# Graph attention with a residual norm on one core: the output bias of the last two tiles added by VectorE, the last tile's power by itself

## The chip, the cores and the metric

The kernel runs on one core of one Trainium2 chip. The metric is the device time of one execution in microseconds (us); the time before is the median of five runs.

## The reference

There are 16 graphs of 1024 nodes with 512 features, one adjacency matrix for all of them, and 8 heads of 64. Cut to what matters:

```python
q = (x @ Wq + bq).reshape(b, n, H, HD)        # k and v likewise
scores = jnp.einsum('bqhd,bkhd->bhqk', q, k) / jnp.sqrt(jnp.float32(HD))
scores = scores + (1.0 - adj)[None, None, :, :] * -1000000000.0
attn = jax.nn.softmax(scores, axis=-1)
out = jnp.einsum('bhqk,bkhd->bqhd', attn, v).reshape(b, n, d)
y = x + out @ Wo + bo
result = (y - mean(y)) / sqrt(var(y) + 1e-5)  # over the 512 features
```

## The kernel before

Nodes are sorted by degree and cut into 8 tiles of 128 queries, for each of 16 graphs: 128 tiles in all. Keys and values are gathered only where the adjacency has an edge, in 560 blocks of 128 rows (35 for each graph). The instructions are issued in an order that the program writes out itself: a loop over steps n (L1097 to L1175), in which each block takes its turn, and in which functions are set down for a later step (`later` puts them in `plan`, `later_last` in `rest`). `total` is the number of blocks, 560, so steps with n of 560 or more lie behind the last block. `fronts` is the list of the projections (q, k, v) still to be done; it runs empty some steps ahead of the last graph. An engine works through its own list in that order, and nothing overtakes.

What this text follows is the end of a tile:

- `normalise` (L977) divides the weighted sum by the denominator; TensorE transposes it (`poT`, L1002), and ScalarE copies it to `oT` (L1006). Ten tiles of two earlier graphs are put off to the end: their `oT` lies in HBM (`spill`) and comes back by `reload` (L773) as `oTs`, for the time when no projections are left.
- `load_y` (L762) brings the residual rows into `Y`, for the late tiles by a DMA on SyncE's queue (L769).
- `finish` (L779) makes the output product `po`: four units, each one matmul of 128x512 in float32 (`product`, L578 to L589). The profile shows each such matmul as two passes, so a tile's product is 8 passes on line L584. When no projections are left (`biased`), a fifth unit goes in after the second: a matmul of a column of ones with the bias `bo_bc` (L868 to L873), 2 passes more on line L869.
- `out` (L784) adds product and residual on VectorE and sums the row in the same instruction (L799); while there are projections an own instruction (L798) adds the product, and L799 the bias. Then, each at its step: `centre` (VectorE, L804), `spread` (ScalarE, squares, L808), `variance` (VectorE, L811), the power to -0.5 (GpSimd), `shift` (VectorE, L817), `norm_out` (ScalarE, L820) and `store` (GpSimd, an indirect DMA to the sorted places, L824).
- The power of a tile is an instruction of its own while there are projections (`power`, L814, 128x1). After that two tiles share one of 128x2 (`powers`, L841): the second of a pair calls it, and both shifts follow it. A first tile that gets no mate is finished by `alone` (L857), which is set down for 6 steps after its `out`.

The last two tiles to be finished are tile 7 of graph 13 (a put-off one, with `oTs`) and then tile 7 of graph 15. Between them, VectorE and TensorE work off the guard's last part (L1056 to L1070: two reductions over `ends`, three small instructions, a transpose `pgt` on TensorE at L1065, and three more that write `flag`). Every engine loads `flag` at the end (L1177) and branches past the general version, which does not run here.

In the last stretch VectorE's list reads: `ends` (L1018, twice), the two shifts of the pair before (L817), L799 of tile 13/7, the guard's instructions, L804 and L811 of tile 13/7, L799 of tile 15/7 and its L804, L811 and the two L817.

Of the kernel before, what the change touches and what calls it, by code (L numbers as in the profile page):

```python
# [14 lines left out]
OP = mybir.AluOpType  # L15
# [145 lines left out]
def kernel(  # L161
# [36 lines left out]
    nc = tc.nc  # L198
# [21 lines left out]
    bo_bc = const.tile([P, D], F32, name="bo_bc")  # L220
# [8 lines left out]
    with ExitStack() as main:  # L229
# [120 lines left out]
        now, plan, rest, urgent = [0], {}, {}, []  # L350

        def later(k, fn):
            plan.setdefault(now[0] + k, []).append(fn)

        def later_last(k, fn):
            rest.setdefault(now[0] + k, []).append(fn)
# [185 lines left out]
        X, XT, SX, KV, VSUM, NRM, Y, OT, PS = {}, {}, {}, {}, {}, {}, {}, {}, {}  # L542
# [35 lines left out]
        def product(name, lhs, w, out):  # L578

            def unit(c):  # L580
                if c == 0:
                    PS[name] = fill_psum(name)
                p = PS[name]
                nc.tensor.matmul(p, lhs()[:, ts(c, P)], w[:, c, :], start=(c == 0), stop=(c == NPAIR - 1))  # L584
                if c == NPAIR - 1:
                    del PS[name]
                    later(1, lambda: out(p))

            return [(PRODUCT, lambda c=c: unit(c), None) for c in range(NPAIR)]  # L589
# [189 lines left out]
        def finish(b, t):  # L779


            biased = not fronts

            def out(p):  # L784
                OT.pop((b, t))
                y = Y[b, t]

                if fronts:
                    st = small.tile([P, 5], F32, name="stats", bufs=6)
                else:  # L790

                    second = bool(half)
                    if not second:
                        half.append([small.tile([P, 2, 5], F32, name="stats_2", bufs=3)])
                    st2 = half[0][0]
                    st = st2[:, int(second), :]
                if not biased:
                    nc.vector.tensor_tensor(y, p, y, op=OP.add)  # L798
                nc.vector.scalar_tensor_tensor(  # L799
                    y, p if biased else bo_bc, 1.0, y, op0=OP.mult, op1=OP.add, accum_out=st[:, 0:1]  # L800
                )

                def centre():
                    nc.vector.tensor_scalar(st[:, 1:2], st[:, 0:1], -1.0 / D, None, op0=OP.mult)  # L804

                def spread():
                    sq = work.tile([P, D], F32, tag="ysq", name=f"ysq_{b}_{t}", bufs=1)
                    nc.scalar.activation(sq, y, AF.Square, bias=st[:, 1:2], accum_out=st[:, 2:3])  # L808

                def variance():  # L810
                    nc.vector.tensor_scalar(st[:, 2:3], st[:, 2:3], 1.0 / D, EPS, op0=OP.mult, op1=OP.add)  # L811

                def power():
                    nc.gpsimd.tensor_tensor(st[:, 3:4], st[:, 2:3], neg_half, op=OP.pow)  # L814

                def shift():
                    nc.vector.tensor_tensor(st[:, 4:5], st[:, 3:4], st[:, 1:2], op=OP.mult)  # L817

                def norm_out():
                    nc.scalar.activation(y, y, AF.Identity, bias=st[:, 4:5], scale=st[:, 3:4])  # L820
                    later(2, store)

                def store():
                    nc.gpsimd.indirect_dma_start(  # L824
                        out=out_rows[b, t], out_offset=bass.IndirectOffsetOnAxis(ap=asked_row[:, t:t + 1], axis=0),
                        in_=y, in_offset=None, element_offset=b * N * D,
                    )
                    del Y[b, t]

                later(1, centre)  # L830
                later_last(2, spread)
                later(3, variance)
                if fronts:
                    later(4, power)
                    later(5, shift)
                    later_last(6, norm_out)
                elif second:
                    mate_shift, mate_norm_out = half.pop()[1]

                    def powers():  # L840
                        nc.gpsimd.tensor_tensor(  # L841
                            st2[:, :, 3:4], st2[:, :, 2:3], neg_half[:, :, None].to_broadcast([P, 2, 1]), op=OP.pow
                        )

                    def shifts():
                        mate_shift()
                        shift()

                    later(4, powers)
                    later(6, shifts)  # L850
                    later_last(6, mate_norm_out)
                    later_last(7, norm_out)
                else:
                    mine = half[0]
                    mine.append((shift, norm_out))

                    def alone():  # L857
                        if half and half[0] is mine:
                            half.pop()
                            power()  # L860
                            later(2, shift)
                            later_last(3, norm_out)

                    later(6, alone)

            units = product(f"po_{b}_{t}", lambda: OT[b, t], W["o"], out)
            if biased:
                def bias():  # L868
                    nc.tensor.matmul(  # L869
                        PS[f"po_{b}_{t}"], ident[:, 0:1].to_broadcast([P, P]), bo_bc, start=False, stop=False  # L870
                    )

                units.insert(2, (PRODUCT, bias, None))  # L873
            return units
# [198 lines left out]
        done, coming, spilled, gathered, fronts, guarded = [], [], [], [0], [], []  # L1073

        total = len(blocks)
# [7 lines left out]
        with tc.manual_schedule():  # L1083
# [13 lines left out]
            while n < total or plan or rest or urgent or done or finishing or spilled or not guarded:  # L1097
# [45 lines left out]
                while credit > 0 or urgent:  # L1143
                    if urgent and not (first_unit and fronts):
                        urgent.pop(0)()
                        continue
                    if (
                        not finishing and len(done) > (LAZY if fronts else 0) and n > loaded.get(done[0], n) + 1
                        and n > last_finish + 1 and not total - 2 <= n < total
                    ):  # L1150
                        finishing = finish(*done.pop(0))
                        last_finish = n
                    units = finishing or fronts
                    if not units:
                        if urgent:
                            urgent.pop(0)()
                            continue
                        break
                    cost, fn, ready = units[0]
                    if ready and not ready():  # L1160
                        if urgent:
                            urgent.pop(0)()
                            continue
                        break
                    del units[0]
                    fn()
                    credit -= cost
                    first_unit = False
# [41 lines left out]
```

## Time and profile before

| what | value |
|---|---|
| median of five runs | 1997.37 us (1994.44 to 1999.51) |
| the profiled execution's own time | 2002.05 us |
| its span, first to last instruction | 2000.2 us |
| mean granted TensorE clock | 0.989 |
| TensorE busy | 1919.3 us, 96% of the span |
| VectorE busy | 1783.9 us, 89% |
| ScalarE busy | 1555.2 us, 78% |
| GpSimd busy | 1296.9 us, 65% |

In the profile PE is TensorE's matmuls, PEld its weight loads, DVE is VectorE, ACT is ScalarE, POOL is GpSimd and SP is SyncE; a "q" behind the name is the engine's sequencer. Times are us from the start of the span unless ns is written. In the list of instructions in order of time, a row gives the start, the time from the first start to the last end, the engine, the line, the operation and its tiles, how many were merged ("x4"), and in brackets the idle time ahead of it and what ended that. In the chain of waits, which is followed back from the last instruction, a row gives the start, the length of that piece of the chain, and whose it is.

### The profile page before, as it was taken

To read this page: it belongs to the slowest core of one execution; us is meant where nothing else is said; L and a number is where in the kernel's file an instruction comes from. 1 tells how busy PE (TensorE), PEld (TensorE's weight loads), DVE (VectorE), ACT (ScalarE), POOL (GpSimd) and SP (SyncE) were. 2 spreads that over 40 slices of the span, in tenths; PEclk is the share of its full clock that TensorE was granted. 3 is DMA by queue.
4 is the path that set the end of the run, shared out by engine and by line. 5 is a ranking of instruction groups with operands and counts; after the bars stand their busy time and mean duration, and the time that the engine had idled before them with its cause. 6 is when DMAs were issued, how large, how long until landed. Compare 5 with 4: busy or idle time off the path is not lost.

```text
span 2000.2 us, 25754 instructions
## 1 busy us (share of the span) xinstructions
PE 1919.3 (96%) x5379; PEld 924.2 (46%) x5379; DVE 1783.9 (89%) x3754; ACT 1555.2 (78%) x6096; POOL 1296.9 (65%) x1205
## 2 busy tenths in 40 slices
PE   8987999999999999999999999999999999889895
PEld 4433454444545454454545445454444545444442
DVE  3788989989899989999998999999799999999895
ACT  3525878878797888879887887979788788878794
POOL 1662565856767686767767686767657675556784
PEclk9999999999999999999999999999999999999998
DMA  6796887888879788888878788888878888988984
GB/s 247 220 340 230 264 304 241 301 270 274 320 260 325 246 295 289 300 290 277 304 260 312 267 304 278 291 302 266 285 257 283 294 303 312 322 280 263 334 308 142
DMA packets 191140, 563.10 MB, mean 282 GB/s; under 512 B 31711, under 2 KB 31739, under 8 KB 190974
## 3 DMA queue, kind: packets, MB, share of 16 engines
q0 software_dynamic: 121632, 403.22, 60.9%
q1 hardware_dynamic: 66736, 153.16, 20.7%
q10 hardware_dynamic: 2606, 4.99, 0.7%
q14 instruction: 122, 1.00, 0.2%
q8 instruction: 44, 0.72, 0.1%
HBM read 442.25 MB, written 143.71 MB: 293 GB/s over the span
## 4 chain that ended last, share of the span: by engine, by line
PE 79%; DVE 10%; issue 4%; DMA 3%; ACT 2%; POOL 1%; POOLq 0%; SPq 0%; DVEq 0%; ACTq 0%
PE po L584 19%; PE pq L584 18%; PE pp L698 13%; PE x L698 9%; PE z L698 9%; PE pxT L555 2%; PE poT L1002 2%; DVE qk L925 2%; PE sum L975 2%; PE sum L974 2%; DVE s L929 2%; DMA kvg<-kv_rows,key_row 1%; ACT pv L949 1%; DVE pv L965 1%; PE pm L646 1%
## 5 line engine op out<-in xcount | busy, mean ns | idle before, releaser
L904 POOL DMA_INDIRECT kvg<-kv_rows,key_row x560 | 636.2, 1136 | 445.6 <-ACT pv L949 116.1
L949 ACT ACTIVATE pv<-kvg,pv 128x64 f32<-128x64 f32 x3552 | 894.7, 339 | 0.5 <-issue 0.4
L584 PE MATMUL pq<-wq,xT 128*128 128x512 f32 x1024 | 480.5, 599 | 3.9 <-issue 1.7
L584 PE MATMUL po<-wo,oT 128*128 128x512 f32 x944 | 438.6, 597 | 4.2 <-DVE y L798 1.9
L929 DVE TENSOR_REDUCE s<-qk 128x8 f32<-128x512 f32 x560 | 380.3, 679 | 6.0
L925 DVE TENSOR_TENSOR qk<-qt,kvg 128x512 f32<-128x512 f32 x464 | 316.9, 683 | 8.3 <-DMA kvg<-kv_rows,key_row 5.0
L584 PEld LDWEIGHTS pq<-wq,xT 128*128 128x128 f32 x1024 | 191.5, 191 | 223.1 <-issue 207.2
L584 PEld LDWEIGHTS po<-wo,oT 128*128 128x128 f32 x944 | 176.2, 191 | 207.3 <-issue 193.2
L698 PE MATMUL pp<-t,s 128*128 128x512 f32 x504 | 237.3, 593 | 8.0 <-DVE s L570 7.0
L698 PE MATMUL x<-b,xT 128*128 128x512 f32 x504 | 237.6, 594 | 0.0
L965 DVE TENSOR_TENSOR pv<-pv,pv 128x520 f32<-128x520 f32 x336 | 232.5, 692 | 0.0
L939 ACT ACTIVATE pv<-s,absent 128x8 f32<-128x8 f32 x464 | 135.6, 293 | 111.0 <-DVE s L929 66.0
L824 POOL DMA_INDIRECT out_dram<-y,asked_row x128 | 149.9, 1171 | 38.8 <-issue 27.3
L888 POOL DMA_INDIRECT qt<-q_rows,asked_row x128 | 142.6, 1114 | 36.7 <-issue 34.8
L594 ACT ACTIVATE sq_k<-kv 128x128 f32<-128x128 f32 x512 | 150.7, 299 | 10.2 <-DVE kv L721 9.0
L698 PEld LDWEIGHTS pp<-t,s 128*128 128x128 f32 x504 | 94.7, 190 | 117.4 <-issue 106.6
L698 PEld LDWEIGHTS x<-b,xT 128*128 128x128 f32 x504 | 95.2, 191 | 113.6 <-issue 109.9
L752 POOL DMA_INDIRECT y<-in_x_dram,asked_row x102 | 115.2, 1129 | 30.6 <-issue 30.0
L698 PE MATMUL z<-b,s 128*128 128x512 f32 x252 | 120.4, 601 | 5.9 <-DVE kv L726 5.9
L898 POOL DMA_INDIRECT qg<-q_rows,query_row x96 | 106.9, 1113 | 27.2 <-issue 24.9
L698 PE MATMUL z<-t,s 128*128 128x512 f32 x252 | 118.7, 593 | 0.1
L698 PE MATMUL pp<-t,xT 128*128 128x512 f32 x252 | 118.4, 592 | 0.0
(194 smaller groups left out, 2613.7 us busy)
## 6 DMA issues: line engine op xcount, KB each, us to landing
kv_rows<-kv SPq DMA_DIRECT2D x128, 512.0 KB
x<-in_x_dram SPq DMA_DIRECT2D x128, 256.0 KB
q_rows<-q SPq DMA_DIRECT2D x128, 256.0 KB
kvg<-kv_rows,key_row POOLq DMA_INDIRECT x560
residual<-y_sorted SPq DMA_DIRECT2D x26, 256.0 KB
y<-residual SPq DMA_DIRECT2D x26, 256.0 KB
adj<-in_adj_dram POOLq DMA_DIRECT2D x8, 512.0 KB
spill<-oT SPq DMA_DIRECT2D x10, 256.0 KB
```

The lines of the kernel that those rows point to most:

```text
L584: nc.tensor.matmul(p, lhs()[:, ts(c, P)], w[:, c, :], start=(c == 0), stop=(c == NPAIR - 1))
L594: nc.scalar.activation(sq, s[:, ts(h, P)], AF.Square, scale=scale, accum_out=sums[:, h:h + 1])
L698: nc.tensor.matmul(R[bank], l[:, ts(c, P)], right[:, c, :], start=(first and c == 0), stop=(c == 1), skip_group_check=True,)
L752: nc.gpsimd.indirect_dma_start(out=y, out_offset=None, in_=x_rows, in_offset=bass.IndirectOffsetOnAxis(ap=asked_row[:, t:t + 1], axis=0), ...
L824: nc.gpsimd.indirect_dma_start(out=out_rows[b, t], out_offset=bass.IndirectOffsetOnAxis(ap=asked_row[:, t:t + 1], axis=0), in_=y, in_offse ...
L888: nc.gpsimd.indirect_dma_start(out=QT[b, t], out_offset=None, in_=q_rows[b % ROWS], in_offset=bass.IndirectOffsetOnAxis(ap=asked_row[:, t: ...
L904: nc.gpsimd.indirect_dma_start(out=KG[n], out_offset=None, in_=kv_rows[b % ROWS], in_offset=bass.IndirectOffsetOnAxis(ap=key_row[:, g:g + ...
L925: nc.vector.tensor_tensor(QK[n], q, KG[n][:, 0:D], op=OP.mult)
L929: nc.vector.tensor_reduce(S[n], QK.pop(n).rearrange("p (h d) -> p h d", d=HD), axis=AX.X, op=OP.add)
L939: nc.scalar.activation(PV[n][:, D:], S.pop(n), AF.Exp, bias=bias)
L949: nc.scalar.activation(pv[:, ts(h, HD)], v[:, ds(D + h * HD, HD)], AF.Copy, scale=pv[:, D + h:D + h + 1])
L965: nc.vector.tensor_tensor(PV[b, t], PV[b, t], pv, op=OP.add)
```

## The change

Behind the last block (step n at or past `total` when `finish` is called) the bias matmul is left out, and VectorE adds `bo_bc` to the residual in `Y` at that moment, which is ahead of the product in the order of the program. L799 then adds the product, as before. A tile whose `out` comes later than step `total + 3` gets its own statistics tile, its own power (L814) and the steps of a single tile.

```diff
         def finish(b, t):
-            biased = not fronts
+            biased = not fronts and now[0] < total
+
+            if now[0] >= total:
+                nc.vector.tensor_tensor(Y[b, t], Y[b, t], bo_bc, op=OP.add)
+
+            fronts_then = bool(fronts)
 
             def out(p):
                 OT.pop((b, t))
                 y = Y[b, t]
 
-                if fronts:
+                single = fronts or now[0] > total + 3
+                if single:
                     st = small.tile([P, 5], F32, name="stats", bufs=6)
                 else:
...
-                if not biased:
+                if fronts_then:
                     nc.vector.tensor_tensor(y, p, y, op=OP.add)
                 nc.vector.scalar_tensor_tensor(
-                    y, p if biased else bo_bc, 1.0, y, op0=OP.mult, op1=OP.add, accum_out=st[:, 0:1]
+                    y, bo_bc if fronts_then else p, 1.0, y, op0=OP.mult, op1=OP.add, accum_out=st[:, 0:1]
                 )
...
-                if fronts:
+                if single:
                     later(4, power)
                     later(5, shift)
                     later_last(6, norm_out)
```

In the lists of instructions that the two programs give their engines, this is all that differs, and it touches the last two tiles alone. TensorE loses the bias matmul of tile 13/7 and that of tile 15/7. VectorE gains an add for each (L785 of the changed kernel): that of 13/7 between L1018 and the two L817 of the pair before, that of 15/7 between the instruction that writes `flag` and L811 of tile 13/7. GpSimd has two powers of 128x1, first that of 13/7 and then that of 15/7, in place of one of 128x2, and both still stand ahead of the last two stores. Tile 15/7 is now normalised (L820) and stored ahead of 13/7; before, 13/7 came first. The lists of ScalarE and SyncE hold the same instructions. The finished tile 13/7 is the first of a pair without a mate, and `alone` finishes it.

## The prediction

> **What bounds the kernel now.** I read the list of instructions that the change moves first, since everything up to about 1973 us is the same program on every engine: only what lies behind that can be won or lost. Then I read, of the profile before, the chain of waits over the last 40 us, the instructions in order of time, the rows of the instructions that come and go, the DMA view around the residual's loads, and last the table of stretches for the granted clock.
>
> The chain of waits tells which engine the end hangs on:
>
> ```profile
> 1973.30 1.72 PE po L584 x4
> 1975.02 0.86 PE po L869 x2
> 1975.88 1.73 PE po L584 x4
> ...
> 1977.63 0.70 DVE y L799 x2
> ...
> 1979.13 0.25 PE pgt L1065
> 1979.38 1.72 PE po L584 x4
> 1981.10 0.86 PE po L869 x2
> 1981.96 1.73 PE po L584 x4
> ...
> 1983.71 0.71 DVE y L799 x2
> ...
> 1985.84 0.72 POOL stats L841
> ```
>
> Three things are to be seen. Both output products are on the chain whole, the bias passes among them. Between them the chain goes over VectorE (L799 of tile 13/7, then the guard's five small instructions) and the guard's transpose on TensorE, so the second product starts when the guard lets it, and that starts from the first product's end. Behind the second product comes a thread with one instruction at a time, in which the power on GpSimd has its whole length.
>
> VectorE's own instructions in order of time, over the same stretch:
>
> ```profile
> 1974.85 0.34 DVE L1018 TENSOR_REDUCE ends<-rden 128x1 f32<-128x64 f32 x2
> ...
> 1977.63 0.69 DVE L799 SCALAR_TENSOR_TENSOR y<-po,y 128x512 f32<-128x512 f32 x1 [2.30 <-PE po L584]
> ...
> 1983.71 0.69 DVE L799 SCALAR_TENSOR_TENSOR y<-po,y 128x512 f32<-128x512 f32 x1 [3.46 <-PE po L584]
> ```
>
> Ahead of each L799 VectorE sat idle, 2.30 and 3.46 us, and the product ended the wait. That is the room for the two adds.
>
> **The bias passes.** Each tile loses two passes, on the chain 0.86 us (the weight loads behind these passes start 0.43 us apart too, so this is not only a modelled end). The first product is the last to arrive at L799, so L799 of 13/7 starts at 1977.63 - 0.86 = 1976.77. The guard's chain follows it unchanged, and the guard's transpose ends at 1979.38 - 0.86 = 1978.52. The second product also needs the copy `oT` (L1006): TensorE's transpose `poT` starts at 1977.43 - 0.86 = 1976.57, takes 0.60, and ScalarE's copy at 0.59 ends about 1977.8, still 0.7 us ahead of the guard. So the second product runs from 1978.52 and takes 3.45 in place of 4.31: it ends at 1981.97, before at 1983.69. **Sum of both: 1.72 us**, all on the chain.
>
> **The first add.** The trace has no add of residual and bias, so its price is bounded by the adds of two 128x512 operands in SBUF that it does have: L994 takes 0.691 at the least, 0.692 in the median, 0.764 at most. I take 0.69. It starts behind L1018 at about 1975.1 and ends at 1975.8. Queued behind it are the two L817 (0.22), then L799: VectorE is free at 1976.0, 0.75 us ahead of the product at 1976.77. The L817 release ScalarE's L820 of tile 15/6 (0.81), which moves from 1975.29 to about 1976.0 and ends at 1976.85; the `oT` copy stands behind it and can't start before 1977.2 anyway. So the add costs nothing on the chain; without this cover it would cost at most its own 0.69 to 0.76, and it can't gain, since nothing it replaces was on VectorE.
>
> The add also brings a wait forward: the residual is wanted at 1975.1, where L799 wanted it at 1977.63. SyncE issued the last two residual loads between 1964.96 and 1965.76, and the DMA view shows traffic of SyncE's queue kind only until about 1969; between 1969.5 and 1975 there is none. So the rows lay there 6 us early, and the wait is nought.
>
> **The second add** stands between the write of `flag` and L811 of 13/7, at about 1979.2 to 1979.9. Behind it wait L811 of 13/7 (which releases the first of the two powers, 4 us before the second needs GpSimd) and L799 of 15/7 at 1981.99. Hidden by the product, with 1.9 us to spare; uncovered it would cost 0.7.
>
> **The power.** Two rows price it:
>
> ```profile
> L814 POOL TENSOR_TENSOR stats<-stats,neg_half x106: 556/587/2062, 224.5 to 1858.6; 128x1 f32<-128x1 f32 x106
> ```
>
> ```profile
> L841 POOL TENSOR_TENSOR stats<-stats,neg_half x11: 717/910/1250, 1882.3 to 1985.8; 128x2 f32<-128x2 f32 x11
> ```
>
> (ns, least, median, most.) Both grow when VectorE is busy beside them; behind the second product it is idle, and there the pair took the least, 0.72. The single one should take its least as well: 0.56. The power of 13/7 goes ahead, at about 1980, where GpSimd is idle. So 0.72 - 0.56 = **0.16 us** less on the chain; from both sides, 0.16 gained and, with the median 0.587 or a stretch such as 0.87 (the last L814 of the run), 0.13 gained to 0.15 lost. I take 0.16, from the row that is as quiet as the tail.
>
> The order of the last two tiles after it (15/7 first) is symmetric: the same shifts, the same two L820, the same two stores in one queue, one step apart as before. Nothing for it. The stretch of 10 us from the last store's issue (1990.20) to the end of the span holds its landing and the program's end and stays.
>
> **Sum.** 1.72 + 0.16 = 1.88 us. Of the profiled execution: 2002.05 - 1.88 = 2000.2, its span 1998.3. That execution lies 4.7 us above the median of the runs; since the tail has no part that differs between executions that I can see, I take the same 1.88 from the median: **1995.5 us**, 0.09% less. The runs differ by 5 us among themselves, and a difference under 0.2% (4 us) can hardly be told from no change: that is the bound for the chances below.
>
> **A rule against the change.** While L994 ran (1974.24 to 1974.93, two operands in SBUF) a store's issue was on GpSimd from 1973.94 to 1974.97; L994 took 0.69 as everywhere. The Trainium skill, SBUF — State Buffer, in "Who interferes with whom", says that a VectorE instruction with two SBUF inputs contends with a GpSimd instruction that reads SBUF, and the later one is blocked whole. By the rule the first add, if it came second to a store's issue, would wait for its end (1976.25); by the row it would not wait. By the rule the sum would be 1.88 - 0.4 = 1.5 us.
>
> **The rivals.**
>
> First, the add is not hidden: it starts only when GpSimd's store issue (1975.28 to 1976.25) is through. It ends at 1976.95, the L817 at 1977.15, and L799 starts 0.4 us after the product. The guard and the second product move with it: 1.88 - 0.4 = 1.5, **1995.9 us**. For it speaks that L841 took up to 1.25 with VectorE busy, so the two do disturb each other; against it that the L994 beside an issue kept its 0.69.
>
> Second, the change doesn't do on the second product what it says: the time won ahead of it is lost waiting for ScalarE's copy, because the add delays L817, so L820, so the copy. Then only one product's 0.86 and the power's 0.16 remain: 1.0 us, **1996.4 us**. It needs the copy to end at 1979.38 in place of 1977.8, 1.6 us late, and L820's delay is 0.7, of which 0.35 is idle time of ScalarE anyway. Little speaks for it.
>
> Third, slower: the clock. The change takes work from TensorE ahead of a gap (1.1 us for the guard). The table of stretches, cut into windows of 3.41 us, the step in which the granted clock changes here (columns: window, its length, busy time and count of PE, PEld, DVE, ACT, POOL, granted clock, DMA share, GB/s):
>
> ```profile
> 1887.04:1890.45 3.41, 0.58 (x3) 0.16 (x1) 3.38 (x9) 0.46 (x3) 3.03 (x3) 1.00 0.96 329
> 1890.45:1893.86 3.41, 1.53 (x6) 1.03 (x7) 3.34 (x16) 2.08 (x10) 2.49 (x4) 0.50 0.90 347
> ...
> 1975.79:1979.20 3.41, 2.33 (x10) 1.09 (x9) 1.39 (x8) 1.45 (x3) 1.43 (x2) 1.00 0.52 199
> ```
>
> A window with 0.58 us of matmuls was followed by one at half clock; one with 2.33 was not, and the one with 1.07 at the very end was. If the window that holds the guard's gap fell under that limit, the last product would run at half clock: 3.45 us become 6.9, and the time is 3.45 - 1.88 = 1.6 us above before: **1999.0 us**. It decides from a limit between 1.07 and 2.33. Against it: the gap itself keeps its length (both ends move by 0.86), and what is cut away is followed by other work at once, so the window keeps about 2.3.
>
> **How the numbers follow.** The forecast 0.82 (1995.5); the add not hidden 0.07 (1995.9); one product only 0.06 (1996.4); slower by the clock 0.05 (1999.0). The bounds of the unknown costs move the forecast by 0.4 at most; the rest of the range is the runs' own scatter, 2.5 us to either side of their middle. So 1993.1 to 1998.0, which leaves out the clock case and the tails. Chances: faster by over 0.2% (under 1993.4) 0.10, by scatter alone; within 0.2% 0.88; slower by over 0.2% (over 2001.4) 0.02.
>
> **What would show it.** In the profile after: both products with 8 passes, 3.45 us on the chain and no bias passes in the last 28 us; the two adds at 0.69 with idle time of VectorE still ahead of each L799, ended by the product; the guard's transpose 0.86 earlier against the first product's start; a power of 0.56 behind the last L811; from the first product's start to the last store's start 1.9 us less than 15.9. The prediction would be wrong if an add has the product waiting in L799's place, if the clock is halved over the last product, if the stretch behind the last store grows, or if anything ahead of 1973 us has another length than by scatter.

## The result and the profile after

The changed kernel takes 1992.8 us (median of 52 runs, 1980.74 to 2003.55), the kernel before 1997.3 us (median of 94 runs, 1986.64 to 2012.95). The ratio is 0.9975, with an interval of 0.9965 to 0.9985: 5 us less (4.5 between the medians), where 1.9 were forecast, and the time lies just under the range (1993.1 to 1998.0). The profiled execution took 1988.1 us with a span of 1986.2, 14 us less than the one of before. So the first question is where these 14 us lie.

The chain of waits of the changed kernel (start, length of the piece, whose):

```profile
1961.27 3.43 PE po L584 x8
1964.70 0.45 PE poT L1008 x4
...
1972.02 0.56 POOL stats L820
...
1973.96 0.96 POOL out_dram L830
...
1975.30 0.96 POOL out_dram L830
```

The first product has its eight passes in one piece. In what lies between the second product and the power the chain now walks along GpSimd's list, where one store and the first power have moved in, and books the rest as "issue"; that is a matter of the walk, and the ends are to be read, not the way. From the start of the first product to the start of the last store it is 1975.30 - 1961.27 = 14.03 us; before it was 1989.23 - 1973.30 = 15.93. The end of the program behind it is 10.9 us, before 11.0. So **1.90 us of the 14 lie in the tail, and 12.0 ahead of it**, where both programs give every engine the same instructions in the same order.

VectorE's instructions in the tail, in order of time:

```profile
1963.08 0.68 DVE L785 TENSOR_TENSOR y<-y,bo_bc 128x512 f32<-128x512 f32 x1
...
1964.74 0.69 DVE L805 SCALAR_TENSOR_TENSOR y<-po,y 128x512 f32<-128x512 f32 x1 [0.84 <-PE po L584]
...
1967.09 0.67 DVE L785 TENSOR_TENSOR y<-y,bo_bc 128x512 f32<-128x512 f32 x1
...
1969.96 0.69 DVE L805 SCALAR_TENSOR_TENSOR y<-po,y 128x512 f32<-128x512 f32 x1 [2.14 <-PE po L584]
```

Both adds lie in VectorE's idle time. Ahead of each L805 (L799 before) it still waits, 0.84 and 2.14 us where it was 2.30 and 3.46, and the product still ends the wait. TensorE's instructions over the two products:

```profile
1961.10 3.60 PE L584 MATMUL po<-wo,oTs 128*128 128x512 f32 x8
...
1966.22 0.27 PE L1071 MATMUL pgt<-ident,gr 128*1 128x128 f32 x1 [1.08 <-DVE gr L1069]
1966.33 3.60 PE L584 MATMUL po<-wo,oT 128*128 128x512 f32 x8
```

Where the 12.0 us lie can be counted matmul by matmul, since the list of matmuls ahead of the tail is the same. In the profile of before the first 100 matmuls take 2.0 us longer, those from the 300th to the 500th (from about 128 to 210 us) 7.3, those from the 1200th to the 4000th 1.8 and the 1000 behind them 1.3; all the rest differs by about 0.1 us or less, and its first matmul starts 0.3 us sooner. The stretch from the 500th to the 900th takes 145.08 or 145.09 us in all twenty traces of this case, whichever kernel and chip. So the time is not smeared over the run; it is lost at a few places.

### The profile page after: what moved, and what is told of

It reads as the page before. It is cut to its first block, busy times and chain, and to the rows that moved or that the text cites. A ratio compares the mean times of both kernels' runs of the same rounds, so it can differ in the third digit from the quotient of the medians.

```text
span 1986.2 us, 25750 instructions
## 1 busy us (share of the span) xinstructions
PE 1915.7 (96%) x5375; PEld 924.7 (47%) x5375; DVE 1786.6 (90%) x3756; ACT 1554.6 (78%) x6096; POOL 1291.2 (65%) x1206
## 4 chain that ended last, share of the span: by engine, by line
PE 75%; DVE 10%; issue 3%; ACT 2%; POOL 1%; DMA 1%; POOLq 0%; DVEq 0%
PE po L584 18%; PE pq L584 18%; PE pp L698 13%; PE z L698 9%; PE x L698 9%; DVE qk L931 2%; PE poT L1008 2%; PE pxT L555 2%; DVE s L935 2%; PE sum L981 2%; PE sum L980 2%; ACT pv L955 1%; DVE pv L971 1%; PE pm L646 1%; DVE y L805 1%
## 5 line engine op out<-in xcount | busy, mean ns | idle before, releaser
L594 ACT ACTIVATE sq_k<-kv 128x128 f32<-128x128 f32 x512 | 150.6, 299 | 9.9 <-DVE kv L721 8.9
L698 PEld LDWEIGHTS pp<-t,s 128*128 128x128 f32 x504 | 95.2, 191 | 117.1 <-issue 107.8
```

The source lines that it names most:

```text
L594: nc.scalar.activation(sq, s[:, ts(h, P)], AF.Square, scale=scale, accum_out=sums[:, h:h + 1])
L698: nc.tensor.matmul(R[bank], l[:, ts(c, P)], right[:, c, :], start=(first and c == 0), stop=(c == 1), skip_group_check=True,)
```

## The experiments

Two theories stand against each other. The **tail theory**: the change is worth 1.9 us in the last 28 us, and the rest of the measured 5 is the scatter of the runs. The **program theory**: the changed program also runs faster ahead of its tail.

In what follows "the tail" is the time from the start of the first of the last two products to the start of the last store. An uncertainty behind "+-" is 1.96 standard errors of a difference of means, worked out from the single runs (copies of one kernel can differ by more, as the zero lines show); the ratios and their intervals are those of the comparisons. In each comparison the kernels share a chip with runs of before.

### One part alone

The kernel before unchanged (no edit), the changed kernel again (no edit), and each part by itself, on one chip.

> The kernel before, unchanged, as a zero line. Both theories: ratio 1.000. Its interval tells what scatter such a comparison carries: if the runs scatter by their start and their half-clock stretches (some 5 us each), the interval reaches 2 to 3 us to either side and its middle can lie 2 us off. In the profile the stretch from the first matmul of the last two products to the start of the last store is 15.9 us, as in the first profile of this kernel, whatever the span.

> The changed kernel once more. Tail theory (the change is worth 1.9 us in the last 28 us and nothing ahead; the other 3 us of the measured 5 are scatter of the runs): 1.9 us below before, ratio 0.9991, with an interval of some 2 us to either side. Program theory (the changed program also runs faster ahead of its tail): 5 us below, ratio 0.9975 again. In the profile, both: 14.0 us from the first matmul of the last two products to the start of the last store.

The bias alone keeps the edit to the bias, and the shared power:

```diff
-                single = fronts or now[0] > total + 3
+                single = bool(fronts)
```

> Only the bias goes to VectorE; the last two tiles share one power as before. Tail theory: 1.72 us less than before, 14.2 us from the first matmul of the last two products to the start of the last store, the shared power at 0.72 us. Program theory: 4 to 5 us less if the lost matmuls carry the rest of the gain, 1.7 if the separate power does.

The power alone is the kernel before with `single` as in the change.

> Only the last tile's power is by itself; the bias stays with TensorE. Tail theory: 0.16 us less than before (no difference that the timing can tell), 15.8 us from the first matmul of the last two products to the start of the last store, the last power at 0.56 us in place of 0.72. Program theory: 3 us less if the separate power carries the rest of the gain, 0.2 if the lost matmuls do.

| kernel | median, us | ratio to before (1975.12) | tail, us |
|---|---|---|---|
| before | 1976.18 | 1.0000 (0.9991 to 1.0009) | 15.92 |
| changed | 1971.74 | 0.9987 (0.9978 to 0.9996) | 14.03 |
| bias alone | 1972.96 | 0.9989 (0.9979 to 0.9999) | 14.22 |
| power alone | 1975.30 | 0.9998 (0.9989 to 1.0006) | 15.76 |

The chain of the kernel with the bias alone:

```profile
1943.93 3.45 PE po L584 x8
...
1949.15 3.45 PE po L584 x8
...
1954.76 0.72 POOL stats L847
...
1958.15 0.97 POOL out_dram L830
```

Both products have 3.45 us where they had 4.31, and the shared power keeps its 0.72. The tail gives 1.70 to the bias and 0.16 to the power (forecast 1.72 and 0.16), and they add up to within 0.03. In the measured times, the intervals of the changed kernel and of the bias alone hold the tail's value and stop short of 0.9975. But on this chip before is 22 us faster than the first comparison, and its runs scatter less.

### The price of a bias matmul, the cover of the adds, and the guard

On another chip, whose runs of before have a median of 1982.19 us: the changed kernel, the bias matmul four times, the changed kernel without the adds, and a version that goes on from the change.

> The changed kernel a third time, in a new comparison. Tail theory: 1.9 us below before (0.9990), within the scatter of such a comparison (1.4 to 1.9 us to either side so far). Program theory: 3 to 5 us below again, as in the two comparisons made. In the profile 14.0 us from the first matmul of the last two products to the start of the last store.

```diff
                 units.insert(2, (PRODUCT, bias, None))
+                if now[0] >= total:
+                    for _ in range(3):
+                        units.insert(2, (0, bias, None))
```

> The kernel before, with the bias matmul of the last two tiles issued four times in place of once (the sum then holds the bias four times; that is the part that differs). Tail theory: six matmuls more at 0.86 us each on the chain, 5.15 us above before (ratio 1.0026), and 21.1 us from the first matmul of the last two products to the start of the last store. Program theory: these matmuls act on more than their own time, so that the two removed ones were worth 4 to 5; then 12 to 15 us above before, or a difference that has nothing to do with their number.

```diff
-            if now[0] >= total:
-                nc.vector.tensor_tensor(Y[b, t], Y[b, t], bo_bc, op=OP.add)
-
```

> The changed kernel without the two adds on VectorE: the last two tiles get no bias at all. Tail theory: the adds are covered by the products, so nothing is gained over the changed kernel: 1.9 us below before and 14.0 us from the first matmul of the last two products to the start of the last store. If the adds cost something after all, that stretch is shorter, by up to 1.4 us. Program theory: a third program, 3 to 5 us below before.

```diff
+            yield
+            yield
             pg = fill_psum("pgt3")
             nc.tensor.transpose(pg[0:1, 0:P], g[:, 0:1], ident)
+            yield
             yield
```

> The changed kernel with the guard's transpose put behind the last product, and its last three instructions on VectorE put into the wait for the squares. Then the last product waits for ScalarE's copy in place of the guard: in the profile of the changed kernel the copy ended at 1965.76 and the product began at 1966.46. Tail theory: 0.7 us less than the changed kernel, 13.3 us from the first matmul of the last two products to the start of the last store, 2.6 us below before. Program theory: no forecast beyond 3 to 6 us below before.

| kernel | median, us | ratio to before | tail, us |
|---|---|---|---|
| changed | 1978.98 | 0.9980 (0.9964 to 0.9997) | 14.04 |
| bias matmul four times | 1989.21 | 1.0030 (1.0011 to 1.0049) | 21.08 |
| changed, no adds | 1979.53 | 0.9981 (0.9964 to 0.9997) | 14.03 |
| changed, guard late | 1977.78 | 0.9969 (0.9954 to 0.9984) | 13.62 |

The chain with the bias matmul four times:

```profile
1954.30 1.72 PE po L584 x4
1956.01 3.43 PE po L869 x8
1959.44 1.73 PE po L584 x4
...
1975.38 0.97 POOL out_dram L824
```

Four matmuls are 3.43 us, so one is 0.86, and the tail grows by 21.08 - 15.93 = 5.15 for six of them, as forecast; the ratio agrees (1.0026 expected). Without the adds the tail is as long as with them: the cover is whole. So no amplification of what TensorE does in the tail is seen: the mean lies 6.4 +-2.6 us above before's, and the 12 to 15 us that the program theory gave to bias matmuls acting on more than their own time are ruled out.

With the guard's transpose behind the last product the tail is 0.42 us shorter than the changed kernel's, not 0.7. TensorE in that run, in order of time:

```profile
1962.72 3.70 PE L584 MATMUL po<-wo,oT 128*128 128x512 f32 x8 [0.68 <-ACT oT L1012]
```

It does wait for the copy, as meant. Measured from L805 of tile 13/7 the product starts 0.51 us earlier than in the changed kernel of this comparison, and takes 3.70 in place of 3.60. Of all versions this has the shortest tail; the measured times can't tell it from the changed kernel (0.6 +-2.3 us between their means).

All four, though, stand 1 to 4 us from where the tail puts them: three of them below it and the one with more matmuls above it. Only the interval of the late guard leaves its tail's value (0.9988) out. So zero lines were wanted beside them.

### Zero lines, on a fast and on a slow chip

No edit: two copies of before and two of the changed kernel, in two comparisons.

> The kernel before, unchanged, as a second zero line on whatever chip this comparison falls. Both theories: ratio 1.000. What it differs from 1 by is the scatter that any of these comparisons carries.

> The changed kernel, in the same comparison as two copies of the kernel before, so that it stands against three times as many runs of before. Tail theory: 1.9 us below all runs of before taken together. Program theory: 4 us below, the mean of the comparisons so far. 14.0 us from the first matmul of the last two products to the start of the last store in both.

> A third zero line: ratio 1.000 by both theories. The two zero lines of this comparison differ from each other by scatter alone; if they lie 2 us apart, a 2 us excess of the changed kernel in one comparison is no evidence.

> The changed kernel once more beside the two zero lines. Tail theory: 1.9 us below all runs of before. Program theory: 4 us below. With the copy beside it the two give 24 runs of the changed kernel.

> The kernel before, unchanged, on one more chip. Both theories: ratio 1.000. A copy of before came out at 0.9989 in one comparison, so up to 0.001 from 1 is expected of it, more where the runs scatter more.

> The changed kernel beside zero lines on one more chip. Tail theory: 1.9 us below the zero lines and before together. Program theory: 4 to 5 us below them. 14.0 us from the first matmul of the last two products to the start of the last store.

> The second zero line of this comparison: ratio 1.000 by both theories.

> The second copy of the changed kernel in this comparison. Tail theory: 1.9 us below the zero lines and before together. Program theory: 4 to 5 us below them.

| median of before's runs | copies of before, ratio | copies of the changed kernel, ratio | changed less the two copies |
|---|---|---|---|
| 1975.20 us | 0.9989 (0.9979 to 0.9999), 0.9993 (0.9984 to 1.0003) | 0.9991 (0.9981 to 1.0000), 0.9991 (0.9980 to 1.0002) | 0.8 us less, +-1.2 |
| 1991.97 us | 1.0006 (0.9991 to 1.0021), 1.0008 (0.9990 to 1.0026) | 0.9972 (0.9955 to 0.9989), 0.9979 (0.9963 to 0.9995) | 6.6 us less, +-2.1 |

The tail is 15.93 or 15.94 us in all four traces of before, and 14.03 or 14.04 in all four of the changed kernel. The measured times are less plain. On the fast chip the two copies of before came out 1.2 +-1.1 us below before's own runs, and on the slow chip 2.2 +-2.0 us above them, though the kernel is the same: such intervals are narrower than the truth, and beside a comparison with all runs of before the table's last column makes less of the change on the fast chip and more on the slow one. Taken against all, as the expectations had it, the copies of the changed kernel gain:

| median of before's runs | gain of the changed kernel against all runs of before, us |
|---|---|
| 1997.3 (first comparison) | 5.0 +-1.9 |
| 1991.97 | 5.3 +-1.7 |
| 1982.19 | 4.7 +-2.0 |
| 1981.93 (the kernels with 120 more instructions, below) | 2.4 +-3.0 |
| 1975.12 | 3.0 +-1.3 |
| 1975.20 | 1.5 +-1.1 |

The tail theory's 1.9 us lie within the uncertainty on both fast chips and on the one of 1981.93 us. On the two slow chips and on the one of 1982.19 they lie 2.8 to 3.4 us below the gain, outside its uncertainty. So the tail theory is right about the tail, and on the slower chips the measured times give some 3 us more; **that this goes with the chip, and not with the copies or the hour, is not shown by six comparisons.**

The traces show where the time ahead of the tail goes. First the clock. The stretch from 23 to 27 us, in the first zero line on the fast chip and in the first copy of the changed kernel beside it (columns as in the prediction's table of stretches), each with a matmul group that both have, from the instructions in order of time:

```profile
23.00:27.00 4.00, 4.00 (x10) 1.73 (x10) 2.29 (x4) 0.70 (x2) 0.00 (x0) 1.00 1.04 394
```

```profile
117.83 1.88 PE L698 MATMUL z<-t,s 128*128 128x512 f32 x4
```

```profile
23.00:27.00 4.00, 4.00 (x6) 1.73 (x7) 2.81 (x6) 0.28 (x1) 0.00 (x0) 0.57 1.04 394
```

```profile
119.81 1.88 PE L698 MATMUL z<-t,s 128*128 128x512 f32 x4
```

The second pair is the changed kernel: its clock fell to half for most of that stretch (0.57), and it is 2.0 us behind at 118 us, and 2.2 us behind where the last products begin. With the tail's 1.9 it ends level with before. Nine of the twenty traces have that window, five of them with before's tail or a variant of it and four with the changed one. In those nine the first 100 matmuls take 42.4 to 42.8 us, in the other eleven 40.6 to 41.1.

What decides it can be read from the traces: in each one, every change of the granted clock lies on one grid of 3.41 us, and the grid falls otherwise against the start of the program in each execution. In the nine traces a step of the grid lies between 22.83 and 23.81 us; in the eleven the steps nearest to that lie at 22.36 us or sooner and at 24.54 us or later. So the window at 23 us is luck of the start and not the program's, and the profile of before in the first comparison had it where that of the changed kernel had not: that is its 2.0 us in the first 100 matmuls. Not every half-clock window costs something: the trace that reaches its last products soonest of all, at 1943.64 us (the first zero line on the fast chip), has one at 106 us, and the 200 matmuls around that place take 82.4 to 82.7 us in every trace, with it or without.

Then stalls. The time from the 300th to the 500th matmul, in us, in all twenty traces:

| median of before's runs | before, or a variant with its bias matmuls | changed, or a variant without them |
|---|---|---|
| 1997 us | 83.0 | 75.8 |
| 1992 us | 81.3, 82.8 | 76.1, 78.0 |
| 1982 us (two chips) | 79.6, 75.8 | 76.0, 75.4, 85.8, 76.1 |
| 1975 us (two chips) | 72.4 to 73.3 in four | 72.4 to 72.8 in four |

On the two slow chips all three traces of before lie above all three of the changed kernel; on the chips of 1982 us there is no such order, and the 85.8 is the version with the late guard, whose list ahead of the tail is the changed kernel's too. VectorE in the first profile of before, and the same instruction in that of the changed kernel:

```profile
154.99 0.69 DVE L726 TENSOR_TENSOR kv<-z,g 128x512 f32<-128x512 f32 x1 [9.95 <-remote]
```

```profile
143.57 0.69 DVE L726 TENSOR_TENSOR kv<-z,g 128x512 f32<-128x512 f32 x1 [0.20 <-issue]
```

and ScalarE in the second zero line on the slow chip:

```profile
155.31 1.07 ACT L559 COPY xT<-pxT 128x512 f32<-128x512 f32 x2 [10.09 <-remote]
```

"remote" means that the profile finds no instruction or transfer of this core that ended the wait. On the fast chips no such wait of TensorE, VectorE or ScalarE of over 0.6 us shows in any trace. On the others the longest come around 145 to 155 us, while the adjacency lists are made, though not in every trace; later ones come in both kernels, the longest of 5.6 us near 1875 us. ScalarE has one of 2.4 us at L594 near 400 us in the three traces of before on slow chips, and one of 3.6 us at the copy `oT` near 372 us in the three of the changed kernel. These two places cost the same: from the 900th to the 1200th matmul it is 111.7 to 111.9 us in those of before and 110.3 to 112.0 in those of the changed kernel, where the fast chips have 107.8 to 108.5. The excess isn't made there.

### A program of another size

That ScalarE's stalls stand at other places in the two kernels suggested the last pair: instructions that never run, added to the general version of before and of the changed kernel.

```diff
+        spare = work.tile([P, D], F32, name="g_spare")
+        for _ in range(40):
+            p = psum.tile([P, P], F32, tag="g_av", name="g_spare_p")
+            nc.tensor.transpose(p, ident, ident)
+            nc.vector.tensor_copy(spare[:, 0:P], p)
+            nc.scalar.copy(spare[:, P:2 * P], p)
```

> The kernel before, with 120 more instructions (40 transposes, 40 copies on VectorE, 40 on ScalarE) in the general version, which is branched past and never runs: every engine executes the same list as before, in a program of another size. Theory of scatter: nothing changes, ratio 1.000 within some 0.001, and on a chip with stalls that the profile gives to no instruction ('remote') they fall at the same places as in the other traces of before (ScalarE's at its line 594 near 400 us). Theory of the program (where these stalls fall depends on the program as a whole, not on what it executes): on such a chip the ratio differs from 1 by 0.001 to 0.003, to either side, and the places move. On a chip without such stalls (span under 1980 us) both expect 1.000, and the run tells nothing.

> The changed kernel with the same 120 instructions that are never executed. Theory of scatter: 1.9 us below before, as without them, and ScalarE's stall on a chip with such stalls at the copy oT near 372 us, as in the other traces of the changed kernel. Theory of the program: on such a chip another difference than the 4 to 6 us that the changed kernel has there, and another place. The tail is 14.0 us by both.

Before with it: 1981.93 us, ratio 0.9995 (0.9977 to 1.0013); the changed kernel with it: 1979.68 us, 0.9993 (0.9976 to 1.0009); the runs of before 1981.93. The chip was one of the middle, the tails are 15.93 and 14.03, and in the two traces the last products begin at 1952.21 and 1952.87, 0.7 us apart. The largest "remote" wait is 0.75 us. ScalarE does wait at `oT` near 373 us, 2.7 us in the one and 2.6 in the other, but there the profile names TensorE as what ended it; from the 900th to the 1200th matmul both take 111.4 us. The changed kernel has its 1.9 us here and no visible excess. With the same instructions added the two kernels stall alike; but neither was run on this chip without them, and a chip that stalls little can't show whether the program decides where stalls fall. **Inconclusive.**

## Why the prediction was wrong

**What held.** The terms of the sum, each in the trace: the bias passes 1.70 to 1.72 us (forecast 1.72), the power 0.56 in place of 0.72 us, the two adds 0.68 and 0.67 and covered, with VectorE idle 0.84 us ahead of the first L805 (forecast 0.75) and 2.14 ahead of the second (1.9). From the start of the first product the guard's transpose comes 0.85 us earlier (5.12 us behind it, before 5.97, by the instructions in order of time). The order of the last two tiles costs nothing. The tail went from 15.93 to 14.03, 1.90 where 1.88 was forecast, and stands at this in every trace.

**What failed** is the step from the tail to the time of the kernel: "everything up to about 1973 us is the same program on every engine: only what lies behind that can be won or lost". The lists are the same; the time they take is not. Of the 14 us between the two profiles 12.0 lie ahead of the tail: 2.0 of them in the half-clock window at 23 us, which is luck of the start, and 7.3 between the 300th and the 500th matmul, where before waits up to 10 us for nothing that the profile shows. Of the measured 5 us, 1.9 are the tail and 3.1 are not. That is the prediction's own last sign of being wrong, "if anything ahead of 1973 us has another length than by scatter".

The range was a second, smaller fault. "The rest of the range is the runs' own scatter, 2.5 us to either side of their middle": five runs spanned 5 us, 94 runs span 26. But the middle of the five held, 1997.37 us against 1997.3, and the tail's 1.9 us below it would have been 1995.4, inside the range. What took the time out of the range is the 3.1 us ahead of the tail, for which the sum has no term. The prediction did give a time under 1993.4 a chance of 0.10, "by scatter alone"; how much of the 3.1 us is scatter is not known.

**What stays open** is why the changed kernel gained more than its tail. That the excess lies ahead of the tail, and mostly between 128 and 210 us, is shown for the first pair of profiles. That the program as a whole (where its code lies, how it is fed) sets the length of the stalls is argued, not shown: the pair meant to test it fell on a chip that stalls little. Chance over so few traces isn't ruled out: three traces against three on the slow chips go one way, but the version with the late guard, on the chip of 1982 us, has VectorE's 11.2 us stall at the same L726 as before, and copies of one kernel in one comparison differ from its other runs by 1 to 2 us. What no run supports is that the executed tail acts back: bias four times cost 5.15 us in the tail and 6.4 +-2.6 in the measured time.

**The rivals.** The add that isn't hidden: not seen, the tail without adds is as long. One product only: not seen, both lost their 0.86. The half clock over the last product: its eight passes took 3.60 us from the first start to the last end, as the first product's did, in every trace of the changed kernel, so the clock was whole there. It was half elsewhere, at the start, which the rival did not look at.

**The rule against the change.** By the Trainium skill, SBUF — State Buffer, "Who interferes with whom", the add contends with a GpSimd instruction that reads SBUF, and the order of issue decides which one is blocked. GpSimd's store issue beside the first add, in the changed kernel, and the one at the same place in the version without adds:

```profile
1963.25 1.36 POOL L830 DMA_INDIRECT out_dram<-y,asked_row  x1 [0.30 <-issue]
```

```profile
1954.39 0.97 POOL L827 DMA_INDIRECT out_dram<-y,asked_row  x1 [0.30 <-issue]
```

The add came first, by 0.17 us, and kept its 0.68; the store's issue took 0.39 us longer, of the 0.51 us in which the two lay side by side. So in this order they contend and the later one pays, though not for the whole of the add, and GpSimd had the time. In the other order, the prediction's case of L994, the store's issue came first by 0.30 us; the later L994 kept its 0.69, and the issue took 1.03, as one does in the changed kernel with VectorE idle (1.04, at 1973.96): there no contention shows. The prediction took from that row that there was no price; it holds for one order only.

## What to carry to other kernels

A tail that every engine enters in the same state can be priced from one trace to a few hundredths of a microsecond, matmul by matmul, and the trace after is where that is checked. Whether the whole kernel's time shows it is another question: where runs scatter by more than the gain, put a copy of the kernel before into the comparison, and on more than one chip, ahead of explaining a number. Equal lists of instructions are no ground for equal times: ahead of the tail the traces of this case differ by up to 30 us. A range should take its scatter from more than five runs on one chip.

## What had not been expected of the hardware

The same program took 1975 to 1997 us from chip to chip. One part of that is made between 128 and 210 us, where the chips of 1975 us need 72.4 to 73.3 us for 200 matmuls and the others 75.4 to 85.8, with waits of up to 11 us on VectorE and ScalarE that no instruction or transfer of the core ends; the stretch behind it takes 145.1 us on all of them. A half-clock window of TensorE at 23 us comes in nine of twenty traces, when a step of the clock's grid of 3.41 us falls between 22.83 and 23.81 us from the program's start, and costs about 2 us; the same kind of window at 106 us costs nothing that shows. A two-operand add in SBUF on VectorE lengthens a store's issue on GpSimd that starts 0.17 us behind it from 0.97 to 1.36 us, and is not lengthened itself.
